# Replacing the rounds of a software-scheduled graph/convolution/GRU kernel by one clock for all streams, with the residual and the weights issued later

## Chip, cores, metric

One core of a Trainium2 chip. The metric is device time in microseconds (us) of one execution. An execution is called slow where it is more than 1.5% above the fastest of the same kernel; only fast ones are compared. PE is TensorE, DVE VectorE, ACT ScalarE, POOL GpSimd.

## The reference, cut

Input x is 32 batches of 512 nodes by 256 channels, adj is 32 masks of 512 by 512. Per batch:

```python
h = jnp.maximum(_layernorm(x, axis=-1), 0.0)              # "norm", then transpose: xc
c = relu(bn1(conv1x1(xc)))                                # "rows"
c = bn2(conv17(c))                                        # "conv": 25 products for each 4 batches
x_conv = relu(c + xc)                                     # "residual"
s = h @ w_se.T + b_se                                     # 3 columns, computed with the messages
A = exp(-dist(s)) * mask
msg = relu(h @ w_msg.T + b_msg)                           # "messages"
x_nmp = A @ msg                                           # "gather"; messages to gather: "graph"
gi = concat([x_conv, x_nmp]) @ w_ih.T + b_ih
gh = h @ w_hh.T + b_hh
r, z = sigmoid(gi_r + gh_r), sigmoid(gi_z + gh_z)         # "gates"
out = x + (1 - z) * tanh(gi_n + r * gh_n) + z * h         # "finish"
```

## The kernel before

The program writes out every instruction in the order in which each engine's queue will hold it; no tool reorders it. A Python generator per stage ("stream") yields how many us of PE it has just issued, and a chooser takes the next stream. Four batches are a group; the 17-tap convolution is done for one group at a time as 25 products, whose results DVE and ACT add up in one buffer `y`.

```python
def load(b):
    XS[b] = front.tile([P, NT, D], F32, name="x_sb", bufs=2)
    nc.sync.dma_start(XS[b], x[b].rearrange("(c p) d -> p c d", p=P))

def begin(b):                       # transposes of the normed x; then x of b+2 is loaded
    for d in range(ND):
        norm_t(b, d)
        if d == ND - 1:
            begun = b + 1
            if b + 2 < B:
                load(b + 2)
                NORMS[b + 2] = norm(b + 2)        # small DVE work, issued in pieces from here on
        yield 0.55, 2.0 * d

def graph(b):
    for c in range(NT):
        messages(b, msg, c)         # 4 matmuls into ps_g (2 banks, shared with rows and gather)
        if c == NT - 1: factors()
        yield 0.93, 0.0 if c < NT - 1 else 4.5    # us of PE, us to leave this stream alone
    ...                             # exponent, 4 masks, 2 gathers

def messages(b, msg, c):
    ps = gps.tile([P, D + 3], F32, name="ps_g")
    matmul_sum(ps, ...)
    nc.vector.tensor_tensor(msg[:, c, :], ps[:, :D], bmsg[:, :D], op=ALU.add)
    nc.vector.tensor_tensor(aug[:, c, :3], ps[:, D:], bmsg[:, D:], op=ALU.add)   # frees ps_g

def summed(g):                      # the sums of a group's 25 products
    for j1 in ORDER:                # (3, 0, 4, 2, 1)
        ...
        sum_all()                   # issues whatever small sums are pending
        if y is None:
            y = cv.tile([P, 3, 3, NZ], F32, name="y")                # one buffer
        z = y[:, 0] if j1 == 3 else cv.tile([P, 3, NZ], F32, name="z")
        nc.vector.tensor_tensor(z[:, 0, :], ps, n3, op=ALU.add)      # the group's first sum
        ...
        if j1 == 3:
            copy(yf[:, 1], zf, 2.0)
            copy(yf[:, 2], zf, 4.0)
    for b in range(g * G, (g + 1) * G):
        for o in range(ND):
            SUMS.append((lambda b=b, o=o: evacuate(y, b, o), 0))     # 8 on ACT, y -> xconv

def gates(b):                       # "then" is issued behind a product's last matmuls
    def residual():
        while b not in evacuated: SUMS.pop(0)[0]()
        xconv = XC.pop(b)[:, :, :N]
        nc.vector.tensor_tensor(xconv, xconv, hT, op=ALU.add)
        nc.scalar.activation(xconv, xconv, AF.Relu)
    ...
    yield from products(ps_r, o, 0, 0, 1, (0, 2), residual, 5.0)

run({"rows": [all_rows(0), 18.0, 0.0], "graphs": [all_graphs(0), 68.0, 0.0]}, 1.2)
while prepare_next(): pass          # the convolution's weights (DVE, ACT), if any are left
for g in range(NG):                 # a round per group
    streams = {"conv": ..., "finish": ...}
    if g + 1 < NG: streams["graphs"], streams["rows"] = ...          # of group g + 1
    if g > 0: streams["gates"] = ...                                 # of group g - 1
    run(streams, 0.4 if g > 0 else 0.7)      # until all but "finish" are used up
```

## Time and profile before

| | before |
|---|---|
| median of 4 fast runs (beside the changed kernel) | 2485.48 us (2483.16 to 2493.44) |
| span of the profiled run, granted clock | 2485.4 us, 0.958 |
| PE / DVE / ACT busy | 93% / 48% / 26% |
| PE work at full speed (the prediction's count; the same matmuls in every run) | 2207 us |

The last row is the measure: the number of matmuls of each kind times the spacing of such matmuls in a dense stretch. What a stage takes beyond it is its **loss**, from waits and from matmuls at a lowered clock. The page's lines are in the prediction.

### The profile page before, as it was taken

How to read it: one execution, taken by the hardware profiler on the slowest of the kernel's cores; microseconds unless marked ns; L12 is line 12 of the kernel's file. 1: busy time of each engine (PE TensorE's matmuls, PEld its weight loads, DVE VectorE, ACT ScalarE, POOL GpSimd, SP SyncE). 2: the span in 40 equal slices, each digit the busy share in tenths (PEclk: the TensorE clock that was granted, in tenths of full speed). 3: DMA queues.
4: the chain of work that ended last, by engine and by line, in shares of the span. 5: the costliest groups of instructions: out<-in, count | busy, mean ns of one | idle time of the engine just before them, and what ended most of it. 6: DMA issues, size and time to landing. Idle time of an engine off the chain costs nothing. (4 is left out here: it accounts for less than half of the span.)

```text
span 2485.4 us, 21807 instructions
## 1 busy us (share of the span) xinstructions
PE 2318.6 (93%) x8224; PEld 1449.6 (58%) x8224; DVE 1193.7 (48%) x1989; ACT 644.4 (26%) x932; POOL 329.0 (13%) x239
## 2 busy tenths in 40 slices
PE   5769979999899999999999998999989999999898
PEld 3447646666566655666556665666656665666443
DVE  6746545643455534544355434564345542555211
ACT  3322232222422223212232123322142222311211
POOL 1000001111011110111001110111101111021122
PEclk8779989999899999999999999999989999999899
DMA  6444343333233333333333333233323332233121
GB/s 233 150 174 149 137 146 104 119 113 106 93 127 111 108 100 98 110 127 98 107 101 115 105 104 125 96 121 118 107 92 124 107 101 87 87 110 105 56 68 34
DMA packets 132279, 277.87 MB, mean 112 GB/s; under 512 B 11984, under 2 KB 61520, under 8 KB 131536
## 3 DMA queue, kind: packets, MB, share of 16 engines
q1 hardware_dynamic: 132176, 276.50, 33.6%
q8 instruction: 65, 1.06, 0.2%
q14 instruction: 38, 0.31, 0.0%
HBM read 213.01 MB, written 63.44 MB: 111 GB/s over the span
## 5 line engine op out<-in xcount | busy, mean ns | idle before, releaser
L93 PE MATMUL ps_c<-x,w 128*128 128x228 f32 x3200 | 684.8, 359 | 24.0 <-issue 18.3
L93 PEld LDWEIGHTS ps_c<-x,w 128*128 128x128 f32 x3200 | 604.0, 191 | 149.7 <-issue 128.3
L634 PE MATMUL ps_acc<-xconv,wih 128*128 128x512 f32 x768 | 369.0, 603 | 13.7 <-ACT xconv L647 13.7
L634 PE MATMUL ps_acc<-hTb,whh 128*128 128x512 f32 x768 | 360.2, 595 | 5.4 <-DMA hTb<-hd 4.9
L634 PE MATMUL ps_acc<-xnb,wih 128*128 128x512 f32 x768 | 362.3, 594 | 0.0
L546 PE MATMUL ps_g<-at,msg 128*128 128x512 f32 x512 | 255.8, 639 | 7.8 <-DVE at L539 7.8
L673 POOL TENSOR_TENSOR o_sb<-hTb,r 128x512 f32<-128x512 f32 x64 | 91.9, 1435 | 1288.7 <-ACT r L668 1250.7
L634 PEld LDWEIGHTS ps_acc<-xconv,wih 128*128 128x128 f32 x768 | 146.6, 194 | 148.6 <-issue 130.1
L634 PEld LDWEIGHTS ps_acc<-hTb,whh 128*128 128x128 f32 x768 | 143.7, 190 | 152.6 <-issue 144.3
L634 PEld LDWEIGHTS ps_acc<-xnb,wih 128*128 128x128 f32 x768 | 142.7, 190 | 136.6 <-issue 135.1
L667 DVE TENSOR_TENSOR r<-ps_acc,r 128x512 f32<-128x512 f32 x64 | 44.2, 690 | 329.6 <-PE ps_acc L634 329.6
L93 PE MATMUL ps_g<-wmsg,hT 128*128 128x259 f32 x512 | 139.7, 403 | 46.9 <-DVE aug L494 38.4
L239 DVE TENSOR_TENSOR x<-x 128x471 f32<-128x471 f32 x200 | 179.8, 916 | 0.0
L546 PEld LDWEIGHTS ps_g<-at,msg 128*128 128x128 f32 x512 | 104.5, 206 | 126.8 <-issue 114.6
L191 DVE BATCH_NORM_STATS2 st<-x_sb 128x6 f32<-128x256 f32 x128 | 52.1, 407 | 250.6 <-DMA x_sb<-in_x_dram 250.6
L242 DVE SCALAR_TENSOR_TENSOR x<-x,x 128x471 f32<-128x471 f32 (+1 forms) x184 | 165.6, 900 | 2.6
L93 PEld LDWEIGHTS ps_g<-wmsg,hT 128*128 128x128 f32 x512 | 100.1, 200 | 99.8 <-issue 82.2
L148 POOL TENSOR_TENSOR rstd<-veps,mhalf 128x4 f32<-128x4 f32 x32 | 35.9, 1123 | 847.7 <-DVE veps L147 847.7
L658 DVE SCALAR_TENSOR_TENSOR r<-ps_acc,vec,r 128x512 f32<-128x512 f32 x64 | 48.0, 750 | 208.4 <-PE ps_acc L634 186.1
L539 DVE TENSOR_TENSOR at<-ps_tr,at 128x512 f32<-128x512 f32 x128 | 88.2, 689 | 111.8 <-PE ps_tr L537 106.0
L664 ACT ACTIVATE z<-ps_acc,brz 128x512 f32<-128x512 f32 x64 | 44.0, 687 | 311.9 <-PE ps_acc L634 311.8
L93 PE MATMUL ps_g<-hT,w 128*128 128x512 f32 x256 | 121.5, 608 | 1.0 <-ACT hT L219 1.0
(98 smaller groups left out, 2041.9 us busy)
## 6 DMA issues: line engine op xcount, KB each, us to landing
w<-wd SPq DMA_DIRECT2D x200, 512.0 KB, 3.6
m_sb<-in_adj_dram SPq DMA_DIRECT2D x128, 256.0 KB, 2.8
x_sb<-in_x_dram SPq DMA_DIRECT2D x32, 512.0 KB, 4.9
hd<-hT SPq DMA_DIRECT2D x32, 512.0 KB, 3.0
nd<-xnmp SPq DMA_DIRECT2D x64, 256.0 KB, 2.1
hTb<-hd SPq DMA_DIRECT2D x32, 512.0 KB, 4.4
xnb<-nd SPq DMA_DIRECT2D x64, 256.0 KB, 2.7
y<-in_x_dram SPq DMA_DIRECT2D x64, 256.0 KB, 4.3
```

Of the source, the lines that this page charges most:

```text
L93: nc.tensor.matmul(ps, lhsT, rhs, start=(i == 0), stop=(i == len(pairs) - 1))
L148: nc.gpsimd.tensor_tensor(dst, t[:, :n], mhalf[:, :n], op=ALU.pow)
L191: nc.vector.bn_stats(st[:, c, :], xs[:, c, :])
L239: nc.vector.tensor_tensor(dst, get(a), get(b), op=ALU.subtract)
L242: nc.vector.scalar_tensor_tensor(dst, a, -2.0, b, op0=ALU.mult, op1=ALU.add)
L539: nc.vector.tensor_tensor(part, ps, part, op=ALU.mult)
L546: nc.tensor.matmul(ps, msg[:, c, d * P : (d + 1) * P], at[:, c, :], start=(c == 0), stop=(c == NT - 1))
L634: nc.tensor.matmul(ps, w[:, at + i, cols(o, g)], hT[:, i, :] if k == 0 else x_in[2 * k - 2 + i], start=(k == of[0] and i == 0), stop=(k == ...
L658: nc.vector.scalar_tensor_tensor(r, ps_h, vec[:, _COL["b_hh"] + 2 * ND + o : _COL["b_hh"] + 2 * ND + o + 1], r, op0=ALU.add, op1=ALU.mult,)
L664: nc.scalar.activation(z, ps_z, AF.Sigmoid, bias=brz[:, ND + o : ND + o + 1])
L667: nc.vector.tensor_tensor(r, ps_n, r, op=ALU.add)
L673: nc.gpsimd.tensor_tensor(t, hT[:, o, :], r, op=ALU.subtract)
```

## The change

Its intent: the rounds end with one graph alone on PE and start with all evacuations at once. If every stream runs through all groups on one clock, there are no such ends. The residual is issued a little behind the evacuation, so that DVE doesn't stand before it, and the weights' work (DVE, ACT) starts only at 18 us of the program's clock, so that the norms of the first batches come first. The program's clock counts us of PE issued; it is not PE's granted clock.

```diff
     def rows(b):
-            if b % G == G - 1 and o == ND - 1:
-                made = b // G + 1
+            if o == ND - 1:
+                rowed = b + 1
+                made = rowed // G
         def residual():
-            while b not in evacuated:
-                SUMS.pop(0)[0]()
             if o == 0:
-                yield from products(ps_r, o, 0, 0, 1, (0, 2), residual, 5.0)
+                yield lambda: b in evacuated          # the stream is held until then
+                yield 0.0, 3.0
+                residual()
+                yield from products(ps_r, o, 0, 0, 1, (0, 2), None, 3.0)
     def prepare_next():
-        return None if next(prepare, "done") == "done" else 700
+        if now < 18.0 or next(prepare, "done") == "done":
+            return None
+        return 700
-    ...                      # run(), the rounds, all_*(g) for one group
+    streams = {              # stream, us of PE per batch, clock at the start (in batches)
+        "finish": (all_finishes(), 1e9, -2.0),
+        "rows": (all_rows(), 1e9, -2.0),
+        "graphs": (all_graphs(), 63.0, -1.15),
+        "conv": (convolution(), 85.5, 0.0),
+        "gates": (all_gates(), 125.0, 1.06),
+    }
+    while streams:           # of the streams neither held nor left alone, the one
+        ...                  # with the lowest clock; its clock advances by pe / rate
```

No matmul, transfer or add is added or removed: PE has 8224 instructions and DVE 1989 in both. The rewrite also alters the streams' rates (gates 129 to 125) and how fast DVE's and ACT's small work is issued beside PE (0.4 to 0.45 per us from the second group's products on).

More of the change, by code (lines that the diff above doesn't have):

```diff
@@ L447, in convolution @@
         wg = (w for _ in range(NG) for w in weights_again())
+        yield lambda: made_w == 25
         for g in range(NG):
@@ L475, in convolution @@
             sums.send(done)
-            yield "group"
     def late_pools():
@@ L570, in load_res @@
             nc.sync.dma_start(XR[b, c], x[b].rearrange("(c p) d -> p c d", p=P)[:, c : c + 2, :])
-    begun = 0
+    begun = rowed = 0
     def begin(b):
@@ L588, in rows @@
     def rows(b):
-        nonlocal made
+        nonlocal made, rowed
         for o in range(ND):
             conv1(b, o)
-            if b % G == G - 1 and o == ND - 1:
-                made = b // G + 1
+            if o == ND - 1:
+                rowed = b + 1
+                made = rowed // G
             yield 1.73
@@ L716 @@
     prepare = weights_first()
-    credit = 0.0
+    credit = now = 0.0
     turn = 0
@@ L750, in pace, with all_graphs, all_rows, all_gates @@
             credit -= 0.06 + 0.0011 * size
-    HOLD = {}
-    def run(streams, rate):
-        now = 0.0
-        ready = {name: 0.0 for name in streams}
-        hold = {name: HOLD.get(name) for name in streams}
-        while set(streams) - {"finish"}:
-            names = [k for k in streams if hold[k] is None or hold[k]()]
-            able = [k for k in names if ready[k] <= now]
-            if able:
-                name = min(able, key=lambda k: streams[k][2] / streams[k][1])
-            else:
-                name = min(names, key=lambda k: ready[k])
-                now = max(now, ready[name])
-            hold[name] = None
-            got = next(streams[name][0], None)
-            if got is None or got == "group":
-                del streams[name]
-            elif callable(got):
-                hold[name] = got
-                if name == "finish":
-                    HOLD[name] = got
-            else:
-                pe, after = got if isinstance(got, tuple) else (got, 0.0)
-                now += pe
-                ready[name] = now + after
-                streams[name][2] += pe
-                pace(pe, rate)
-    def all_graphs(g):
-        for b in range(g * G, (g + 1) * G):
-            if g > 0:
+    def all_graphs():
+        for b in range(B):
+            if b < G:
+                yield lambda: begun > b
+            else:
+                yield lambda: rowed > b - G
+                yield from begin(b)
+            yield from graph(b)
+    def all_rows():
+        for b in range(B):
+            if b < G:
                 yield from begin(b)
             else:
-                yield lambda: begun > b
-            yield from graph(b)
-    def all_rows(g):
-        for b in range(g * G, (g + 1) * G):
-            if g == 0:
-                yield from begin(b)
-            else:
-                yield lambda: freed >= g - 1 and begun > b
+                yield lambda: freed >= b // G - 1 and begun > b
             yield from rows(b)
-    def all_gates(g):
-        for b in range(g * G, (g + 1) * G):
+    def all_gates():
+        yield lambda: late is not None
+        for b in range(B):
             yield from gates(b)
@@ L809 @@
             nc.sync.dma_start(wflat[:, c, k0:k1, :], conv2_w[:, c, k0:k1, :])
-    run({"rows": [all_rows(0), 18.0, 0.0], "graphs": [all_graphs(0), 68.0, 0.0]}, 1.2)
-    while prepare_next():
-        pass
-    conv, finishes = convolution(), all_finishes()
-    for g in range(NG):
-        streams = {"conv": [conv, 85.5 * 0.96, 0.0], "finish": [finishes, 1e9, 0.0]}
-        if g + 1 < NG:
-            streams["graphs"] = [all_graphs(g + 1), 63.0 * 0.8, 0.0]
-            streams["rows"] = [all_rows(g + 1), 14.0, 9.0]
-        if g > 0:
-            streams["gates"] = [all_gates(g - 1), 129.0, 6.0]
-        run(streams, 0.4 if g > 0 else 0.7)
-    run({"gates": [all_gates(NG - 1), 129.0, 0.0], "finish": [finishes, 1e9, 0.0]}, 1.0)
-    for _ in finishes:
-        pass
+    streams = {
[5 more added lines that the diff above has]
+    }
+    clock = {name: at for name, (_, _, at) in streams.items()}
+    ready = {name: 0.0 for name in streams}
+    hold = {name: None for name in streams}
+    while streams:
+        names = [k for k in streams if hold[k] is None or hold[k]()]
+        able = [k for k in names if ready[k] <= now]
+        if able:
+            name = min(able, key=lambda k: clock[k])
+        elif names:
+            name = min(names, key=lambda k: ready[k])
+            now = max(now, ready[name])
+        else:
+            pace(1.0, 1.0)
+            continue
+        hold[name] = None
+        got = next(streams[name][0], None)
+        if got is None:
+            del streams[name]
+        elif callable(got):
+            hold[name] = got
+        else:
+            pe, after = got if isinstance(got, tuple) else (got, 0.0)
+            now += pe
+            ready[name] = now + after
+            last = name == "conv" and at_product >= 25 * (NG - 1)
+            clock[name] += pe / streams[name][1] * (0.9 if last else 1.0)
+            pace(pe, 2.0 if at_product == 0 else 0.8 if at_product < 25 else 0.45)
 _OUT = ((32, 512, 256), "float32")
```

## The prediction

> **What bounds the kernel now.** I read the page first (engines, the 40 slices), then the stretches by stage, then the timeline around the places where the stretches lose time.
>
> ```profile
> PE 2318.6 (93%) x8224; PEld 1449.6 (58%) x8224; DVE 1193.7 (48%) x1989; ACT 644.4 (26%) x932; POOL 329.0 (13%) x239
> ...
> PE   5769979999899999999999998999989999999898
> ...
> PEclk8779989999899999999999999999989999999899
> ```
>
> TensorE (PE) is the bound, VectorE (DVE) and ScalarE (ACT) are half idle. But 93% busy is not 93% of its best: the clock row falls below full in the first slices and wherever the PE row dips, every five slices or so.
>
> To see what is to be had I counted its work at full speed, from spacings in dense stretches of the trace: 4 matmuls of a gate product start every 1.72 us (0.429 each), 8 of the convolution every 1.54 (0.192), 4 of the messages every 0.87 (0.2185), 4 transposes every 0.44 (0.109), 8 of the exponent's every 1.07 (0.134). With the page's counts: 3200 x 0.192 + (2304 gates + 512 gather + 256 rows) x 0.429 + 512 x 0.2185 + 1184 x 0.109 + 256 x 0.134 = 2207 us. The span is 2485, so **278 us are lost**, to waits and to matmuls at a lowered clock. The change removes no matmul, so its gain is a share of these 278.
>
> The same count over the order of instructions, up to the end of each group's 25 convolution products, set beside the times of those ends in the trace (158.6, 326.6, 617.8, 913.2, 1209.8, 1507.6, 1800.4, 2096.6, 2328.1, 2485.4) gives the loss by stage: start 86; group 0: 37; groups 1 to 6: 16, 20, 21, 22, 17, 20; group 7: 11; tail 29. The stretches (length, then busy us of PE, PEld, DVE, ACT, POOL, clock, DMA share, GB/s; cut a few us beyond some of those ends) show them:
>
> ```profile
> 0.00:158.60 158.60, 102.94 (x308) 53.46 (x308) 99.29 (x225) 59.54 (x107) 9.82 (x21) 0.79 0.54 200
> 158.60:331.00 172.40, 146.89 (x662) 117.77 (x663) 99.15 (x196) 33.91 (x59) 4.43 (x4) 0.92 0.42 142
> ...
> 617.80:917.00 299.20, 289.31 (x1042) 181.30 (x1041) 146.54 (x245) 80.58 (x114) 40.30 (x28) 0.98 0.33 107
> ...
> 2328.30:2485.40 157.10, 132.87 (x328) 59.81 (x326) 30.98 (x37) 29.84 (x36) 33.08 (x26) 0.93 0.16 50
> ```
>
> A whole group is 276 us of work in some 296. Where the 20 go is seen in the timeline of PE after a group's last product (617.8), then of ACT at the same time:
>
> ```profile
> 631.22 3.09 PE L537 MATMUL ps_tr<-ident,m_sb 128*128 128x128 f32 x12 [1.27 <-ACT at L530]
> 636.91 8.82 PE L546 MATMUL ps_g<-at,msg 128*128 128x512 f32 x16 [0.78 <-DVE at L539]
> ...
> 663.49 2.66 PE L93 MATMUL ps_c<-x,w 128*128 128x228 f32 x8 [3.67 <-issue]
> ```
>
> ```profile
> 657.04 2.37 ACT L413 ACTIVATE xconv<-y,bn_shift,bn_scale 128x513 f32<-128x513 f32 x2
> ...
> 664.29 5.53 ACT L413 ACTIVATE xconv<-y,bn_shift,bn_scale 128x513 f32<-128x513 f32 x5
> ```
>
> At the end of a round the last graph is left alone with its chain (exponent, mask, gather) because convolution and gates are used up; the gather then takes 8.82 us where 16 dense matmuls take 6.87. When the new round starts, the gates need the evacuated convolution, and eight evacuations (9.2 us) stand together on ACT. From 617.8 to 672 there are 54 us for 37 us of work: 17 of the group's 20 lost. Between rounds PE has nothing to wait for (all 50.00 us busy in most 50 us stretches).
>
> The tail waits once for the last sums and evacuations, then 1.29 us a batch for the residual:
>
> ```profile
> 2341.58 3.78 PE L634 MATMUL ps_acc<-xconv,wih 128*128 128x512 f32 x4 [9.87 <-ACT xconv L647]
> ...
> 2376.72 1.98 PE L634 MATMUL ps_acc<-xconv,wih 128*128 128x512 f32 x4 [1.29 <-ACT xconv L647]
> ```
>
> And at the start DVE stands before the weights' transfer, with the evacuation of the messages behind it (DVE, then PE):
>
> ```profile
> 21.77 1.76 DVE L291 SCALAR_TENSOR_TENSOR g<-wraw 128x1536 f32<-128x1536 f32 x1 [8.03 <-DMA wraw<-in_conv_w_dram]
> ```
> ```profile
> 25.88 2.06 PE L93 MATMUL ps_g<-wmsg,hT 128*128 128x259 f32 x4 [9.10 <-DVE aug L494]
> ```
>
> **What the Trainium skill says.** "TensorE: Matmul & The Clock Gate", What's actually happening: the array's clock is halved by default and after about 3.4 us of idleness, and released by activity. The trace agrees: after the 9.87 us wait in the tail the next 8 gate matmuls took 6.2 us (2341.58 to 2347.80), not 3.43. So a wait costs its length and some 2 to 3 us more. The same page, Architectural detail: ACT and DVE queues are strictly first in, first out, and PE pulls only weight loads ahead. The two fences above agree: 8.03 us of DVE before one transfer became 9.10 us of PE. "ScalarE: Activation LUTs", What ACT_TABLE_LOAD costs: about 1283 ns for a switch; the trace has 1.28 us. Both orders hold 50 loads, so nothing changes there.
>
> **The change, part by part.** I compared the orders of the two kernels on PE, DVE and ACT.
>
> Streams without rounds. At the ends of groups 1 to 5 the graphs are now a batch ahead (17 begun, 16.5 gathered at product 75; before 16 and 15), the rows of the next group are done, in one run of 8 (13.7 us of dense PE), and the gates still have a quarter batch of the old group to do. No graph stands alone there: its exponent, masks and gather lie between convolution and gate products. So of the 17 us at a boundary most goes. What stays is the evacuation: the eight stand together on ACT in the new order too (9.2 us), with a message's relu (0.6) and the residual's relu (1.06) behind them. Between them and the first gate product that needs the residual, PE has 10.7 us of other work (a convolution half 1.54, six messages' matmul instructions 2.6, then 1.54, 1.72, 0.87, 0.87, 1.54). ACT starts about 3 us late, as DVE finishes the sums (three of 1.57). 3 + 9.2 + 0.6 + 1.1 = 13.9 against 10.7: a wait of some 3 us, with 2 us of low clock after it. With the 2 to 3 us a group loses anyway I put 8 in place of 20: the five groups 2 to 6 lose 40 in place of 99. **Gain 59.**
>
> Between group 0 and 1 it doesn't help: convolution still waits for the rows of batch 7, and in the new order one graph (exponent, 16 masks, gather) again stands alone. 17 in place of 16; group 0 stays at 37, since its waits (7.7, 5.4, 5.7, 6.5 us at 175, 224, 272, 320 for a message's evacuation, DVE standing before an x transfer that was just issued) have the same order around them.
>
> Group 7 and tail. All graphs are done when group 7 starts, and convolution runs 10% faster than the gates, so at its end 11 gate products (19 us) of the old group are left: more than the 13.5 us from the last product to the first evacuated residual (2328.1 to 2341.6). The 9.87 us wait and its 2.8 us of low clock go. The three waits of 1.29 stay: residual still follows the last mix on DVE (0.69 + 1.23 + 1.07 against 1.72 of hidden product). Also the end: from the last product to the end 12 us. Tail 29 to 16, group 7 11 to 8. **Gain 16.**
>
> Weights later. The 8.03 us of DVE before the weights go. But norm of batch 2 stands in the place: its transfer lands 11.6 us after its issue at 15.1, so DVE waits until 27 anyway. Then DVE does norm 3, norm 4, the first weights (7 + 2.7 us) and norm 5 ahead of graph 0's masks, each norm behind its own transfer. By the order and the durations of before I get graph 0's gather done at 75 (before 69), graph 1's at 104 (96), graph 2's at 138 (122), weights at 145 and the first product at 152 (158.6). Then 62 us of work are done, in place of 73, as graph 3 moves beside the convolution. Loss 90 in place of 86. **Cost 4.**
>
> Sum: 2207 + 90 + 37 + 17 + 40 + 8 + 16 = 2415; as my start is reckoned serially and is rather long, I take **2413 us**, 2.9% less.
>
> **Rivals.** (a) The evacuation wait grows instead of shrinking: eight evacuations and sigmoid, relu and exponent of three streams are in one queue, and the two accumulators of the gates fill. For it: the 3.67 us stall at 663.49 is of this kind. Against: ACT is busy 26%, and PE has gates of the old group to do. It would leave 15 us a group: 2450. (b) The start goes badly: DVE has 52 us of weights' work, now pressed against the end, and convolution may not start before the 25th weight. If the first product comes at 170, 2432. If it goes well (145), 2406. (c) The boundaries vanish wholly, 3 us a group, as in the middle of a round: 2390. (d) Nothing gained, as PE is 93% busy: spoken against by the clock row and the count of 2207.
>
> **Range and chances.** (a) and (b) together would give 2470, (c) with a good start 2380. I take 2375 to 2450. Faster by over 2% means under 2436, 23 us above my number: 0.76. Within 2%: 0.22. Slower: 0.02, as no work is added.
>
> **What would show it.** Right: the PE row without its dips after slice 10; clock 1.0 in most slices there; groups of 280 to 286 us; no PE wait near 10 us at the last convolution; three waits of 1.3 us in the tail. Wrong: a PE wait over 5 us on an ACT residual or a mask at each boundary; a first product after 165 us; PE waits inside groups for DVE standing before an x transfer.

## More of the kernel before

The waits of PE in the kernel before (us in total, times, longest):

```profile
PE ps_g L93 <- DVE aug L494: 38.4, 15, 9.1
...
PE ps_acc L634 <- ACT xconv L647: 13.7, 4, 9.9
```

The first is a message's matmul that waits until DVE has emptied one of the two `ps_g` banks (line 494, the last of the two adds). The second is a gate product that waits for the residual.

## The result, and the profile after

Ratios here and below are the mean time of one kernel's fast runs over that of the kernel before in the same rounds, so not quite the ratio of the medians quoted.

| | before | after |
|---|---|---|
| median | 2485.48 us | 2586.88 us (2584.81 to 2587.76, 4 runs) |
| ratio | | 1.0401 (95%: 1.0377 to 1.0425) |
| span, clock of the profiled run | 2485.4, 0.958 | 2583.0, 0.947 |

The change made it 4.0% slower; the prediction was 2.9% faster. The page of the changed kernel (busy time, the 40 slices of PE, the granted clock):

```profile
PE 2327.6 (90%) x8224; PEld 1462.6 (57%) x8224; DVE 1186.3 (46%) x1989; ACT 641.2 (25%) x932; POOL 353.4 (14%) x239
...
PE   4678979799989999999989999999998999899998
...
PEclk8789979999999999999999999999999999999999
```

PE is busy 9 us longer than before (2327.6 against 2318.6, at a lower mean clock) and idle 89 us longer. Dips to 8 remain (slices 12, 21, 31, 35), and slice 8, which falls in group 1, is a 7 where the kernel before has a 9. Group 1 and group 2 of the changed kernel as stretches (length, busy us of PE, PEld, DVE, ACT, POOL, clock, DMA share, GB/s):

```profile
323.10:697.30 374.20, 329.23 (x1179) 206.02 (x1179) 170.37 (x310) 98.63 (x144) 45.71 (x27) 0.93 0.32 108
697.30:1005.70 308.40, 285.37 (x1030) 181.64 (x1030) 138.96 (x240) 79.22 (x112) 42.70 (x28) 0.97 0.31 104
```

Group 1 has 305 us of work in 374, group 2 276 in 308. The waits of PE after:

```profile
PE ps_g L93 <- DVE aug L494: 112.6, 25, 8.0
PE ps_acc L635 <- ACT xconv L646: 31.0, 10, 6.5
```

Waits for a message's evacuation went from 38.4 to 112.6 us. DVE is 46% busy and an evacuation takes it 0.6 us, so DVE isn't short of time: it is the order of its queue. The Trainium skill says that ACT and DVE are strict FIFO ("TensorE: Matmul & The Clock Gate", Architectural detail), and here the trace shows it in three forms. A "stand" below is time in which DVE waits for something slow, with the rest of its queue behind it. Each form is shown as DVE's timeline (start, length, instruction, idle time before it and what ended that), then PE's.

**Form 1: behind the norm of a batch whose x has just been requested.** The changed kernel, group 1:

```profile
562.76 0.43 DVE L191 BATCH_NORM_STATS2 st<-x_sb 128x6 f32<-128x256 f32 x1 [7.29 <-DMA x_sb<-in_x_dram]
...
565.63 0.42 DVE L493 TENSOR_TENSOR msg<-ps_g,bmsg 128x256 f32<-128x256 f32 x1
```

```profile
566.26 1.57 PE L93 MATMUL ps_g<-wmsg,hT 128*128 128x259 f32 x4 [4.54 <-DVE aug L494]
```

`begin` requests x of batch b+2 and its norm goes on DVE at once. DVE stands 7.29 us before the transfer; the messages' adds are behind the norm; both `ps_g` banks are full; PE's next instruction is another message. The kernel before has the same stand, only longer (8.91 us; in all 250.6 us against 199.1), and at this place loses nothing by it:

```profile
605.32 0.43 DVE L191 BATCH_NORM_STATS2 st<-x_sb 128x6 f32<-128x256 f32 x1 [8.91 <-DMA x_sb<-in_x_dram]
...
609.92 0.42 DVE L493 TENSOR_TENSOR msg<-ps_g,bmsg 128x256 f32<-128x256 f32 x1
```

```profile
602.77 1.04 PE L93 MATMUL ps_g<-wmsg,hT 128*128 128x259 f32 x4
603.65 1.88 PE L634 MATMUL ps_acc<-xnb,wih 128*128 128x512 f32 x4
605.37 1.70 PE L93 MATMUL ps_c<-x,w 128*128 128x228 f32 x8
606.91 1.04 PE L93 MATMUL ps_g<-wmsg,hT 128*128 128x259 f32 x4
```

Its messages are 4 us apart with gate and convolution products between them, which need nothing of DVE just then.

**Form 2: behind the next group's first sum.** The changed kernel where group 2 starts (DVE, ACT, PE):

```profile
725.57 0.63 DVE L381 TENSOR_TENSOR y<-ps_c,n 128x456 f32<-128x456 f32 x1 [8.79 <-ACT xconv L413]
...
727.20 0.39 DVE L493 TENSOR_TENSOR msg<-ps_g,bmsg 128x256 f32<-128x256 f32 x1
```

```profile
716.82 8.72 ACT L413 ACTIVATE xconv<-y,bn_shift,bn_scale 128x513 f32<-128x513 f32 x8 [0.28 <-DVE y L358]
```

```profile
717.92 1.91 PE L93 MATMUL ps_g<-wmsg,hT 128*128 128x259 f32 x8
727.81 1.63 PE L93 MATMUL ps_g<-wmsg,hT 128*128 128x259 f32 x3 [7.97 <-DVE aug L494]
```

The first sum writes the single `y` and so waits until ACT's eight evacuations have read the old one. Messages' adds stand behind it. (The last view ends within its four matmuls, so it counts three.) The wait list names DVE line 494 as releaser; the cause, line 381, is six DVE instructions ahead of it and waits for ACT.

**Form 3: behind work piled up by such a stand,** the residual among it. The changed kernel at 868 us:

```profile
869.48 0.43 DVE L191 BATCH_NORM_STATS2 st<-x_sb 128x6 f32<-128x256 f32 x1 [6.66 <-DMA x_sb<-in_x_dram]
...
872.36 1.22 DVE L645 TENSOR_TENSOR xconv<-xconv,hTb 128x1024 f32<-128x1024 f32 x1
...
874.20 0.43 DVE L493 TENSOR_TENSOR msg<-ps_g,bmsg 128x256 f32<-128x256 f32 x1
```

```profile
874.84 2.07 PE L93 MATMUL ps_g<-wmsg,hT 128*128 128x259 f32 x4 [5.33 <-DVE aug L494]
```

I sorted each message wait over 0.4 us by the DVE stand that overlaps it by more than 0.05 us (none: form 3, which is thus the remainder):

| message waits, us (times) | before | after |
|---|---|---|
| 1, norm | 19.6 (3) | 41.7 (8) |
| 2, first sum | 0 | 30.2 (5) |
| 3, piled up | 9.0 (8) | 40.7 (12) |
| weights' transfer at the start | 9.1 (1) | 0 |

A wait can also cost clock behind it: the messages at 874.84 took 2.07 us, at 602.77 they took 1.04.

### The profile page after: what moved, and what is told of

Read it like the earlier page. It is cut to its first block, busy times and chain, and to the rows that moved or that the text cites. A ratio compares the mean times of both kernels' runs of the same rounds, so it can differ in the third digit from the quotient of the medians.

```text
span 2583.0 us, 21766 instructions
## 1 busy us (share of the span) xinstructions
PE 2327.6 (90%) x8224; PEld 1462.6 (57%) x8224; DVE 1186.3 (46%) x1989; ACT 641.2 (25%) x932; POOL 353.4 (14%) x239
## 4 chain that ended last, share of the span: by engine, by line
PE 74%; DVE 5%; DMA 4%; ACT 4%; issue 1%; SPq 0%; POOL 0%; POOLq 0%; ACTq 0%
PE ps_acc L635 37%; PE ps_c L93 18%; PE ps_g L546 7%; PE ps_g L93 6%; DMA x_sb<-in_x_dram 4%; ACT xconv L413 2%; PE ps_tr L537 2%; PE ps_tr L560 1%; PE ps_g L526 1%; DVE xconv L645 1%; DVE x L239 1%; DVE st L191 1%; ACT hT L219 1%; PE ps_tr L218 0%; ACT xconv L646 0%
## 5 line engine op out<-in xcount | busy, mean ns | idle before, releaser
L93 PE MATMUL ps_c<-x,w 128*128 128x228 f32 x3200 | 691.7, 362 | 25.5 <-DVE y L381 11.2
L635 PE MATMUL ps_acc<-xconv,wih 128*128 128x512 f32 x768 | 376.2, 614 | 31.0 <-ACT xconv L646 31.0
L672 POOL TENSOR_TENSOR o_sb<-hTb,r 128x512 f32<-128x512 f32 x64 | 102.2, 1596 | 1490.5 <-ACT r L667 1352.2
L93 PE MATMUL ps_g<-wmsg,hT 128*128 128x259 f32 x512 | 153.8, 442 | 116.2 <-DVE aug L494 111.2
L546 PE MATMUL ps_g<-at,msg 128*128 128x512 f32 x512 | 244.2, 617 | 6.2 <-DVE at L539 6.1
L93 PEld LDWEIGHTS ps_g<-wmsg,hT 128*128 128x128 f32 x512 | 108.5, 219 | 164.6 <-issue 145.2
L242 DVE SCALAR_TENSOR_TENSOR x<-x,x 128x471 f32<-128x471 f32 (+1 forms) x184 | 174.9, 950 | 3.0
L239 DVE TENSOR_TENSOR x<-x 128x471 f32<-128x471 f32 x200 | 163.6, 837 | 0.3
L148 POOL TENSOR_TENSOR rstd<-veps,mhalf 128x4 f32<-128x4 f32 x32 | 44.8, 1401 | 719.6 <-DVE veps L147 719.6
L191 DVE BATCH_NORM_STATS2 st<-x_sb 128x6 f32<-128x256 f32 x128 | 51.8, 405 | 199.1 <-DMA x_sb<-in_x_dram 199.1
```

The source lines that it names most:

```text
L93: nc.tensor.matmul(ps, lhsT, rhs, start=(i == 0), stop=(i == len(pairs) - 1))
L148: nc.gpsimd.tensor_tensor(dst, t[:, :n], mhalf[:, :n], op=ALU.pow)
L191: nc.vector.bn_stats(st[:, c, :], xs[:, c, :])
L239: nc.vector.tensor_tensor(dst, get(a), get(b), op=ALU.subtract)
L242: nc.vector.scalar_tensor_tensor(dst, a, -2.0, b, op0=ALU.mult, op1=ALU.add)
L546: nc.tensor.matmul(ps, msg[:, c, d * P : (d + 1) * P], at[:, c, :], start=(c == 0), stop=(c == NT - 1))
```

## The experiments

The **main theory** that came out of this: the loss is DVE's queue order (forms 1 and 2), with messages issued in bunches. **Rivals**: the evacuation and residual at the boundary as such (my prediction's rival), the late start, or the loss of rounds itself. Every result was correct; the kernel before ran beside them with medians of 2484.48 to 2488.10 us.

### Holding the norm back (e1 on the changed kernel, e2 on the kernel before)

```diff
-                    NORMS[b + 2] = norm(b + 2)
+                    (NORMS if b < G else LATER)[b + 2] = norm(b + 2)
             if c == NT - 1:
                 factors()
+                if b + 2 in LATER:
+                    NORMS[b + 2] = LATER.pop(b + 2)
```

From batch 4 on, the norm goes to DVE only behind the batch's four messages.

> The kernel after, with one thing changed from batch 4 on: the norm of batch b+2 may be issued on VectorE only after the four messages of batch b have been issued, not at once after its transfer. Theory N (messages' evacuations stand on VectorE behind a norm that waits for a transfer issued a moment before; 112.6 us of TensorE waits named after L494 in 25 places, about 20 of them from batch 4 on, each with some 2 us of low clock): waits under L494 fall to under 30 us, time 2440 to 2475. Rival E (evacuations and residual on ScalarE at the group ends): waits under L494 are merely where it shows, time over 2550. Rival S (the later start, 11 us): over 2570.

Measured: 2453.12 us, ratio 0.9874 (0.9855 to 0.9892). The same edit on the kernel before:

> The same edit on the kernel before. Its waits under L494 are 38.4 us, about 27 of them from batch 4 on in 5 to 6 places. Theory N: 2485 less 27 and about 10 of clock, 2445 to 2460. If the rounds had no such waits to lose, 2480 or more.

Measured: 2434.34 us, ratio 0.9792 (0.9769 to 0.9816). This one change to DVE's order takes 134 us off the changed kernel and 50 off the kernel before, a little more than expected there.

### A third x buffer (e3), the weights' delay (e4)

e3 takes away what the norm waits for and leaves the order alone: in the traces of the changed kernel and of e3, PE, DVE and ACT run the same instructions in the same order. (x of batch 2 is also loaded at the start.)

```diff
-        XS[b] = front.tile([P, NT, D], F32, name="x_sb", bufs=2)
+        XS[b] = front.tile([P, NT, D], F32, name="x_sb", bufs=3)
-                if b + 2 < B:
-                    load(b + 2)
-                    NORMS[b + 2] = norm(b + 2)
+                if b + 3 < B: load(b + 3)
+                if b + 2 < B: NORMS[b + 2] = norm(b + 2)
```

> The kernel after with three x buffers in place of two, each transfer issued a batch earlier; VectorE's order is as in after. Theory N in its narrow form (it is the transfer's wait, not the norm's own 4 us of VectorE work before the messages): nearly as good as the held norm or better, as batches 0 to 3 gain too: 2430 to 2475, waits of VectorE for x under 40 us (199 in after). If the norm's own work in front of the messages were the cost: over 2540.

Measured: 2439.21 us, ratio 0.9820 (0.9802 to 0.9838): 148 us less than the changed kernel. DVE's stands before x, 199.1 us in 24 in the changed kernel, are gone but for one:

```profile
DVE st L191 <- DMA x_sb<-in_x_dram: 5.9, 1, 5.9
```

Of the 148 us, 63 are waits for a message (112.6 to 49.5) and 20 waits for the residual (31.0 to 11.0); PE is also busy 44 us less (2327.6 to 2283.6), at a higher mean clock.

e4 drops `now < 18.0`:

> The kernel after without the delay of the weights (they may be issued from the start). Tells what the later weights are worth alone: first convolution product at 162.9 us in after. If the delay costs, 2560 to 2578 and a first product near 150; if it pays, 2588 or more.

Measured: 2566.97 us, ratio 1.0327 (1.0304 to 1.0350). The first convolution product comes at 140.8 us in place of 163.0 with the same work done (62 us). Up to there DVE stands 22.3 us before x transfers in the changed kernel and 2.7 us in e4: the weights' work fills those stands when it is there. So the delay costs 20 us.

### Both, and the rounds with the third buffer (e5, e6)

> The changed kernel with three x buffers (each x transfer issued one batch earlier) and without the delay of the weights. If the two costs found so far stand in different stretches of the run, they add: the third buffer took 2586.9 to 2439.2 (147.7 us), the delay's removal 2586.9 to 2567.0 (19.9 us), so 2419 us. If the weights at once only fill the front with work that the x loads left room for, the third buffer has already taken it: 2435 to 2440.

Measured: 2425.23 us, ratio 0.9760 (0.9739 to 0.9780); the delay is worth 14 us here, not 20.

> The kernel before with three x buffers, its rounds unchanged. Theory (norm before its transfer on VectorE): rounds suffer from it too, in 15 waits of 38.4 us, so about as much as holding the norm back gave: 2430 to 2440. Rival (the rounds have messages far enough apart, and the third buffer only changes traffic): 2470 to 2485. Compared with the changed kernel with three buffers (2439.2) it says what streams without rounds are worth once the norm is out of the way.

Measured: 2433.05 us, ratio 0.9790 (0.9765 to 0.9815). So with form 1 gone from both, one clock was only 8 us ahead of rounds, and something else still ate its gain.

### Messages apart (e7)

```diff
-            yield 0.93, 0.0 if c < NT - 1 else 4.5
+            yield 0.93, 3.5 if c < NT - 1 else 4.5
```

> The changed kernel with one thing altered: between the four messages of a batch the graph stream lets 3.5 us pass, so that other streams' matmuls come between; the norm stands where the change has it. If bunching is what turns VectorE's wait into TensorE's wait, the waits for a message's evacuation fall from 112.6 us to under 50 and the time to 2480 to 2530. If the norm alone decides it (whoever comes after it waits), the waits stay over 90 us and the time over 2560.

Measured: 2527.10 us, ratio 1.0160 (1.0136 to 1.0185). The message waits fall to 4.9 us in 2. PE's largest wait in e7 is another:

```profile
PE ps_acc L635 <- ACT xconv L646: 58.9, 18, 6.1
```

108 us of message waits went and the time fell by 60: bunching is what turns DVE's stands into message waits, but the stands are still there, and other consumers meet them.

### The old residual (e8 with e5's edits, e9 alone)

```diff
-                yield lambda: b in evacuated
-                yield 0.0, 3.0
-                residual()
-                yield from products(ps_r, o, 0, 0, 1, (0, 2), None, 3.0)
+                yield from products(ps_r, o, 0, 0, 1, (0, 2), residual, 5.0)   # and the while loop
```

> The changed kernel with three x buffers and the weights at once, and with the residual back where the kernel before had it (inside the first products, evacuations forced, 5.0 us allowed). If the later residual is the gain that the change meant it to be, this is slower than the same kernel with the new residual by 10 to 20 us. If it is only moved waiting (31.0 us in 10 waits in the changed kernel against 13.7 in 4), the two are within 5 us.

Measured: 2385.36 us, ratio 0.9598 (0.9579 to 0.9618): 40 us less than e5, which neither case of the expectation had.

> The changed kernel with only the residual put back where the kernel before has it; two x buffers, weights late, norm as the change has it. The old residual took 39.9 us (2425.2 to 2385.4) off the kernel whose norm was already cured. If its cost is its own, it takes about as much here: 2587 to 2540 or 2555. If the residual only hurts by delaying messages that the norm delays anyway, the gain is hidden here: 2575 to 2590.

Measured: 2485.95 us, ratio 1.0004 (0.9965 to 1.0044). Undoing the residual's part alone gives 101 us: it undoes the whole loss. I had expected 32 to 47. Message waits are 63.1 us in 19: form 1 is still 35.5 in 7, form 2 one of 2.8, form 3 24.7 in 11.

Why does the residual's place matter so much, when waits for the residual itself are 31 us? The start of group 2 on DVE in e5 (new residual), then in e8 (old):

```profile
646.79 0.63 DVE L381 TENSOR_TENSOR y<-ps_c,n 128x456 f32<-128x456 f32 x1 [8.78 <-ACT xconv L413]
...
648.42 0.39 DVE L493 TENSOR_TENSOR msg<-ps_g,bmsg 128x256 f32<-128x256 f32 x1
```

```profile
637.56 0.39 DVE L493 TENSOR_TENSOR msg<-ps_g,bmsg 128x256 f32<-128x256 f32 x1
...
646.04 0.63 DVE L381 TENSOR_TENSOR y<-ps_c,n 128x456 f32<-128x456 f32 x1 [6.09 <-ACT xconv L413]
```

The stand is in both; in e5 the message is behind it, in e8 ahead. The residual's part (its place, the hold and the two pauses of 3 us in the gates' stream) shifts where the graph's messages fall; which of these does it was not tested, except the forced evacuation (e10). Form 2 is 29.1 us in e5 and 2.8 in e8.

### One half of the residual's part (e10)

e5 with `while b not in evacuated: SUMS.pop(0)[0]()` in place of the hold.

> The kernel with three x buffers and weights at once (2425.2), with one half of the residual's part undone: the first batch's evacuations are issued at once when its gates start, as before, but the residual itself stays issued 3 us behind them and ahead of the first products. If the loss comes from evacuations left in the queue of small work until all eight are flushed in a row in front of the next group's first sum (8.7 us on ScalarE, VectorE standing 8.8 us before it), this alone brings most of the 40 us back: 2385 to 2400. If it comes from where the residual stands relative to the products, or from the gates stream being held, it stays at 2415 to 2425.

Measured: 2423.18 us, ratio 0.9748 (0.9717 to 0.9778). The second case of the expectation, so evacuations left in the queue are not the cause. Form 2 is still 25.4 us in 3.

### Everything, with messages apart (e11)

> The fastest kernel so far (three x buffers, weights at once, old residual: 2385.4) with the messages 3.5 us apart in addition. Its waits for a message's evacuation are 26.9 us in 11; if spacing removes them without making others, 2360 to 2375. In the changed kernel the spacing took such waits from 112.6 to 4.9 us but left the time 60 us below, not 108, because other waits (residual 58.9 us in 18) took their place; if that repeats here, 2385 to 2410.

Measured: 2413.10 us, ratio 0.9713 (0.9681 to 0.9745): 28 us slower than e8. A loose distance isn't a cure.

### Taking form 2 away (e12, e13)

A second `y` was not tried. The first sum can go to the small buffer `z` instead; ACT copies it into `y`, where it follows the evacuations in ACT's own order:

```diff
-            z = y[:, 0] if j1 == 3 else cv.tile([P, 3, NZ], F32, name="z")
+            z = cv.tile([P, 3, NZ], F32, name="z")
             if j1 == 3:
+                copy(yf[:, 0], zf, 1.0)
```

> The kernel with three x buffers and weights at once (2425.2), new residual kept; the next group's first sum goes to a buffer of its own and is copied later by ScalarE, so VectorE no longer stands 8.8 us before the old evacuations. If the residual's 40 us come from messages that stand behind this wait, 2380 to 2395, and the waits for a message's evacuation fall from 54.9 to about 25. If they come from the residual's pauses themselves, 2415 to 2430.

Measured: 2364.13 us, ratio 0.9509 (0.9490 to 0.9528), from its three fast runs (2362.89 to 2364.67). The profiled run was slow (4026.63 us, clock 0.555), so its trace is not used; e19 below repeats the kernel. It went below what I had expected: 61 us less than e5.

> The same edit on the kernel with the old residual (2385.4), where only 2.8 us of message waits stand behind that wait. If the alignment is all there is, little is left to gain: 2375 to 2388, level with the run before; the extra copies on ScalarE (some 1.7 us a group) cost nothing as ScalarE is a quarter busy.

Measured: 2374.94 us, ratio 0.9552 (0.9534 to 0.9571): 10 us from the edit, at the lower end of what I expected. With form 2 gone the new residual is 10 to 12 us faster than the old one (e12 and e19): the residual's part is a small gain that had run into a wait worth 61.

### Shifting the graphs' stream (e14, e16)

```diff
-        "graphs": (all_graphs(), 63.0, -1.15),
+        "graphs": (all_graphs(), 63.0, -1.25),
```

> The kernel with three x buffers and weights at once (2425.2), new residual kept, nothing of its edits undone; only the graphs' clock starts 0.10 of a batch earlier, so that in groups 2 to 6 the compiled order has the batch's messages before the next group's first sum instead of behind it. If alignment is the cause, 2385 to 2400; if the residual's place costs by itself, 2415 to 2430.

Measured: 2499.52 us, ratio 1.0051 (1.0031 to 1.0072). A clear miss: 74 us slower than e5. PE's waits in e14, then PE's timeline where group 3 starts:

```profile
PE ps_c L93 <- DVE y L381: 53.5, 6, 11.9
...
PE ps_g L93 <- DVE aug L494: 15.0, 5, 11.5
```

```profile
949.55 4.89 PE L93 MATMUL ps_c<-x,w 128*128 128x228 f32 x24
961.60 3.41 PE L93 MATMUL ps_c<-x,w 128*128 128x228 f32 x8 [7.17 <-DVE y L381]
```

The messages do miss the stand (DVE still stands 9.66 us before line 381), but convolution products now come in a row there and wait for the first sum themselves. Rows bunch as well: 42 waits of under 1 us, 36.6 together, for ACT to empty their bank. A shift moves the collision; it doesn't remove it.

> The changed kernel (2586.9) with only the graphs' clock started 0.10 of a batch earlier; two x buffers, weights late, new residual. 30.2 us of its message waits stood behind the first sum and 39.3 us behind work that VectorE had piled up, 36 us before the x transfer. If the whole loss of groups 2 to 6 (132.7 us) is alignment of messages with VectorE's waits, a shift alone moves the time by tens of us: 2490 to 2540. If not, 2570 to 2590.

Measured: 2584.10 us, ratio 1.0394 (1.0376 to 1.0411): no change, the second case of the expectation. Its trace shows why: waits for a message fell from 112.6 to 46.8 us and those for the residual from 31.0 to 11.0, but convolution products now wait for the first sum (11.2 to 55.6 us) and rows for ACT (0.9 to 37.5). It is e14's collision again, and here the two sides cancel.

### How much form 2 costs alone, and what one clock is worth (e17, e18, e19)

> The changed kernel (2586.9) with only the first sum's own buffer; norm, two x buffers, late weights and new residual as the change has them. 30.2 of its 112.6 us of message waits stood behind that wait. If the two stands add: 147.7 us of the third buffer plus about 61 of this, so 2520 to 2535 here. If the norm's stand hides this one, because messages that no longer wait for the one wait for the other, 2550 to 2585.

Measured: 2539.60 us, ratio 1.0212 (1.0191 to 1.0233): 47 us, between the two cases. PE's order in its trace is that of the changed kernel, instruction by instruction. Form 1 hides part of form 2.

> The kernel before with three x buffers (2433.1) and the first sum's own buffer, rounds kept. In rounds nothing of the graph stands behind the first sum at a boundary (11.5 us of message waits in 4, 10.1 of them at the start), so little to gain: 2422 to 2433. The fastest kernel (2364.4) has the same two edits, no rounds, the new residual; the distance is then what streams without rounds are worth with VectorE's stands gone: about 60 us, of which some 16 is the earlier start.

Measured: 2434.70 us, ratio 0.9794 (0.9773 to 0.9816). The edit does nothing in rounds, where no message wait was of form 2.

> The fastest kernel again, unchanged, for a profile in the fast state: 2362 to 2368, waits for a message's evacuation about 12 us in 2 (all in the first 30 us), clock 0.98, loss per group in groups 2 to 6 under 6 us.

Measured: 2362.86 us (2361.74 to 2364.20), ratio 0.9506 (0.9484 to 0.9528). The message waits were 24.2 us in 10, not 12 in 2; the slow trace of e12 had shown fewer. But 12.2 of them is one wait at 28 us, and the other nine are under 2.3 us each. Page, waits, and group 2 in e19:

```profile
PE 2262.3 (96%) x8224; PEld 1421.6 (60%) x8224; DVE 1198.6 (51%) x1989; ACT 648.2 (27%) x940; POOL 364.3 (15%) x239
...
PE   5799899999999999999999999999999999999898
...
PEclk8789899999999999999999999999999999999999
```

```profile
PE ps_g L93 <- DVE aug L495: 24.2, 10, 12.2
```

```profile
606.20:886.50 280.30, 277.72 (x1029) 175.86 (x1029) 142.99 (x240) 79.99 (x113) 45.14 (x28) 1.00 0.35 115
```

Group 2 takes 280.3 us, in place of 308.4, at a clock of 1.00, and ACT's eight evacuations still take 8.84 us in a row beside it.

### The loss by stage

Loss in us, recounted from the traces with the prediction's spacings, up to the first convolution product, then to the end of each group's 25 products, then to the end of the span:

| | start | g0 | g1 | g2 to g6 | g7 | tail |
|---|---|---|---|---|---|---|
| before | 87 | 36 | 16 | 99 | 11 | 30 |
| predicted for after | 90 | 37 | 17 | 40 | 8 | 16 |
| after | 101 | 28 | **69** | **137** | 15 | 25 |
| e9, old residual alone | 101 | 30 | 61 | 53 | 5 | 24 |
| e3, third x buffer | 92 | 5 | 33 | 62 | 14 | 24 |
| e17, first sum apart | 101 | 29 | 61 | 107 | 6 | 24 |
| e8, e5 with the old residual | 81 | 2 | 31 | 29 | 8 | 24 |
| e18, rounds, both stands cured | 83 | 4 | 15 | 80 | 12 | 30 |
| e19, one clock, both cured, weights at once | 78 | 2 | 27 | **16** | 4 | 25 |

The expectation of e16 used an earlier count (132.7 for the 137, 39.3 for the 40.7 of form 3).

## Why the prediction was wrong

- **What bounds the kernel, and that 278 us are to be had.** Right. PE at full speed is 2207 us in every trace; e19 leaves 152 of loss.
- **Streams without rounds, gain 59 in groups 2 to 6.** The mechanism was right: with DVE's two stands gone, one clock loses 16 us there and rounds 80 (e19 against e18), 64 us. But the changed kernel lost 137. **The step that failed** is "Between them and the first gate product that needs the residual, PE has 10.7 us of other work": I asked only who waits for ACT's evacuations among the gates and reckoned 3 us, and for the rest of a group I kept its old 2 to 3 us. DVE's first sum waits for the evacuations too (8.79 us), with the messages behind it (form 2), and the stands before x catch messages as well (form 1). From 137 us there, the third buffer alone leaves 62 (e3) and the first sum alone 107 (e17); with both and the weights at once 16 stay (e19). With form 1 gone, taking form 2 away gave 61 us (e12 against e5).
- **Waits of messages behind the norm.** I had seen them, in group 0, and wrote that "group 0 stays at 37" because its order stays. It measured 28. What I didn't ask is what the new order does to messages in all other groups. In the kernel before other products lie between its messages, but it isn't spared either: the third buffer takes 52 us off it (e6), 31 of them in group 0. In the changed kernel it takes 148. This wait stood in the last sentence of the prediction as a sign of error, and not in its sum.
- **Group 1, 17.** Measured 69: six message waits of 3.0 to 6.7 us between 355 and 655 us, four of form 1 and two of form 3. With the cures 27 remain, more than the 15 of cured rounds: that fits the one graph that the prediction saw alone there, but no run tests it.
- **Residual.** I put its waits at some 3 us a boundary and three of 1.29 us in the tail. The three were there (2474, 2508, 2541 us), and five of 2.4 to 6.5 us stood between 1424 and 1883 us. I gave its part no effect on other streams. Alone it is 101 us (e9), of which 83 in groups 2 to 6. That it acts by where messages fall is shown for form 2 (e12 against e13); for the rest it is argued from the waits of e9.
- **Weights later, cost 4.** 20 us (e4), 14 with the third buffer. DVE's wait to 27 us was right (27.26), but the first product came at 163, not 152. I compared the start with that of the kernel before (loss 86 to 90; it measured 87 to 101) and so missed that one clock by itself makes the start better (79 in e4: 140.8 less 62) and the delay makes it 22 us worse, as nothing fills DVE's stands.
- **Tail, 29 to 16.** 25. The 9.87 us wait became 6.10, although the gates had 20.6 us of old products left, as reckoned (19): the first residual came 26.9 us after the last product, not 13.5.
- **"Slower: 0.02, as no work is added."** That is the wrong ground. A change of order can add waits without adding work.
- **Rivals.** A wait of 15 us at each boundary (a) was nearest, but it put the wait on gates that need ACT, where it was messages behind DVE. The late start (b), 163 us against 152 with the same 62 us of work, is 11 us of the error of 174.

Singly, the third buffer (148), the weights (20) and the first sum (47) make 215 us, together 224. Still open: which part of the residual's edit shifts the messages, how its 101 us split beyond the waits listed at e9, and what the altered rates of the streams do.

## What to carry to other kernels

When an order is rewritten for a scheduled kernel, list on each in-order engine the instructions that wait for something slow (a transfer, another engine's series, a buffer with one copy), and look up what the new order puts right behind them; a stand that costs nothing now may be there only by the luck of the present order. Remove such a stand by its cause (a third buffer, a first write to another buffer) before tuning offsets: in e14 and e16 an offset moved the loss from one consumer to another, while the two cures, with the weights' delay dropped, took 224 us and made the change worth what it was meant for. The releaser that a wait list names can be innocent: go up its queue to the instruction with the idle time.

## What the Trainium skill lacked or had wrong

- "TensorE: Matmul & The Clock Gate", Architectural detail, has the strict FIFO of DVE and ACT, and the runs agree, but not the consequence: 46% busy DVE cost PE 112.6 us, as its stands before transfers and before ACT were passed on to PE.
- The same page, "HAM oscillation — how this bites in real kernels", gives "no PE-idle gaps >~3.4µs" as the rule. Shorter gaps cost the clock here. In e5 four messages took 1.12 us after a gap of 3.05 and 2.07 after one of 4.26 just behind it:

```profile
1800.37 1.12 PE L93 MATMUL ps_g<-wmsg,hT 128*128 128x259 f32 x4 [3.05 <-DVE aug L494]
1805.74 2.07 PE L93 MATMUL ps_g<-wmsg,hT 128*128 128x259 f32 x4 [4.26 <-DVE aug L494]
```

The second gap runs from 1801.48 to 1805.74, but the trace's record of the granted clock is at half from 1801.81 on, 0.33 us into it: it can't be put down to the length of the second gap. In e8, four messages at 925.49 took 2.06 us after a wait of 2.83; before that wait lay 5.9 us of dense work and then a gap of 1.95. The clock was granted at 0.53 from 925.5 to 929.0.

- "Perfetto Trace Analysis", Optimization Strategy, says to find what updates the semaphore that a gap waits for and to make it start sooner or finish faster. Here that names an add of 0.15 us. To start it sooner was right (e8 does), but nothing it reads was late: the section lacks the step from the releaser up its own queue (8.79 us before line 381).
- I found on no page that a change to one issuing stream moves other streams' collisions: the residual's part (its place, hold and two pauses of 3 us) was worth 101 us.
